# A planner that hands out PSUM banks by what open products can still finish, and a row factor applied in one instruction

## The chip, the cores and the metric

The kernel runs on one core of one Trainium2 chip. The metric is the device time of that core in microseconds. A core has a matmul engine (TensorE, PE), three engines for elementwise work (VectorE, DVE; ScalarE, ACT; GpSimd, POOL) and a queue from which transfers are issued (SyncE, SP). Each engine works through its own instructions in the order in which they were built, and waits at an instruction until the semaphores that it names are raised.

## The reference, cut to what matters

`x` has shape (128, 128, 256): 128 graphs of 128 nodes with 256 features each. `adj` holds one 128 x 128 matrix of 0 and 1 for each graph. Four layers follow each other, each with a residual and a layer norm:

```python
# layer 0: three steps of a gated graph network, the same GRU weights in all three
for i in range(3):
    m = einsum('bnd,de->bne', h, weight[i]);  aggr = einsum('bst,bsd->btd', A, m)
    h = gru_cell(aggr, h, w_ih, w_hh, b_ih, b_hh)
x = layernorm(x + h)
# layers 1 to 3: graph attention
Wh = x @ W.T;  e = leaky_relu(Wh @ a1 [:, None] + Wh @ a2 [None, :], 0.2)
alpha = softmax(where(adj == 0, very_negative, e));  x = layernorm(x + alpha @ Wh)
```

All of it is in fp32.

## The kernel before, in words

**Groups and steps.** Four graphs form a group (`G = 4`), 32 groups make the batch. `gru(g, stage)` emits the three GRU steps of a group, `gat(g, ...)` its three attention layers. In a GRU step the hidden state and the aggregate are held transposed, features in partitions. L630 makes the aggregate, and `strassen` forms the gate products at L572 with seven products of half blocks in place of eight. It is called twice in each step: `rz` has two gates and both sides (hidden and aggregate), so a product there is four matmuls; `nn` has two matmuls a product. The half blocks' sums come from `sums` (L542, on POOL or DVE).

**The banks of one form.** A call of `strassen` is called a form here. It opens three PSUM banks, `bx`, `by` and `bz`, of which there are five (tag `gate`). Products go on accumulating in a bank after what was in it has been copied out: `bx` takes A11, is copied by ScalarE (L638 for `rz`; L642 and L645, two instructions for two halves, for `nn`), takes S2, is copied again, and so on. VectorE adds two banks to a copied part (L577). A form that has begun thus needs all its three banks before it can give them back.

**Attention.** The score of a neighbour is a row that is spread over the partitions (L761 transposes it, L768 broadcasts it on POOL). L784 adds the mask and takes the maximum, L788 and L805 are the leaky ReLU and the exponential. The scores are then turned by a transpose over DMA: `turned` packs halves of the words (L466), issues the transpose from SP (L467) and unpacks (L470; the copies stand in the profile under L363, L365 and L461). L854 multiplies the scores with the features and L865 with the weights; L871 divides and adds the residual. Attention layers 1 to 3 do without a full layer norm between them: a factor for each row, `rstd`, is carried on, and in the last two of the three layers the turned scores are multiplied by it (`scaled`, L812 to L818). The last four groups (`LAST = 4`) transpose on TensorE instead of by DMA.

**The planner.** None of this is emitted directly. `plan.op(engines, fn, reads, writes, prio, ...)` records each operation with a price in ns for each engine that may do it. `order()` then plays the program through with those prices, picks for each operation an engine, a start and the slots of its buffers, and the instructions are emitted in the order of these starts. What matters here:

- On TensorE an operation counts as ready only when its inputs from other engines have been there for `MARGIN` ns by the plan.
- `own` holds, for a GRU part (first dictionary) and an attention part (second), how many slots of a tag are kept for the oldest part that still needs some; younger parts are given what is over. `spare` computes it.
- `PASSES` is the number of further rounds in which the due times found in the last round become priorities; the shortest plan of all rounds is kept.
- An operation with `port=BOTH` is not set on DVE while POOL holds the port by the plan, nor the other way.

A planned wait of TensorE is no instruction: on the chip each engine goes on as soon as the semaphores allow.

Of the kernel before, what the change touches and what calls it, by code (L numbers as in the profile page):

```python
# [13 lines left out]
ALU = mybir.AluOpType  # L14
AX = mybir.AxisListType

P = 128
D = 256
KC = D // P
G = 4  # L20
# [10 lines left out]
class Buf:  # L31


    def __init__(self, tag, *shape):
        self.tag, self.shape = tag, shape
        self.left = 0
        self.slot = None
        self.owner = None
        self.at = None


class Op:
# [7 lines left out]
class Plan:  # L50
# [10 lines left out]

    RUSH = 1.5
    RATHER = 600
    MARGIN = 50

    def __init__(self, slots, own):
        self.free = {t: list(range(n)) for t, n in slots.items()}
# [28 lines left out]
        self.ops.append(o)  # L96

    AHEAD = 1000000
    PASSES = 2

    def order(self):

# [41 lines left out]
    def once(self):  # L144
        import heapq
        for o in self.ops:
            o.missing, o.users = len(o.deps), []
            o.at, o.when = {}, {}
            for b in o.bufs:
                b.left, b.slot, b.owner = 0, None, None  # L150
        for o in self.ops:
            for b in o.bufs:
                b.left += 1
            for d in o.deps:
                d.users.append(o)
        idle = {"PE": 0, "ACT": 0, "DVE": 0, "POOL": 0, "SP": 0}
        ready = {e: [] for e in idle}
        done, seq, now = [], 0, 0
        arrived, started, running, leaving = [], set(), [], []
        held, coming, port = {}, {}, 0  # L160
        for o in self.ops:
            for b in o.bufs:
                if b.owner is None:
                    b.owner = o.group
                    coming[o.group, b.tag] = coming.get((o.group, b.tag), 0) + 1
        oldest = {t: min(g for g, t2 in coming if t2 == t) for t in self.free}

        def spare(g, t):

            while oldest[t] < g and not coming.get((oldest[t], t)):  # L170
                oldest[t] += 1
            first = oldest[t]
            if g <= first:
                return len(self.free[t])
            return len(self.free[t]) - max(0, min(self.own[first % 2].get(t, 1) - held.get((first, t), 0), coming[first, t]))

        def release(o):
            for e in o.engines:
                margin = self.MARGIN if e == "PE" else 0
                when = max([t + self.DELAY.get((e2, e), self.LATENCY[e2]) + (margin if e2 != e else 0) for e2, t in o.at.items()],  # L180
                           default=0)
                o.when[e] = max(when, o.earliest)
                heapq.heappush(arrived, (max(when, o.earliest), o.prio, e, o))

        for o in self.ops:
            if not o.missing:
                release(o)
        while len(done) < len(self.ops):
            while running and running[0][0] <= now:
                _, _, o, e = heapq.heappop(running)  # L190
                for b in o.bufs:
                    b.left -= 1
                    if not b.left:
                        heapq.heappush(leaving, (now + self.LATENCY[e] + o.lag, seq, b))
                        seq += 1
                for u in o.users:
                    u.missing -= 1
                    u.at[e] = max(u.at.get(e, 0), now + o.lag)
                    if not u.missing:
                        release(u)  # L200
            while leaving and leaving[0][0] <= now:
                b = heapq.heappop(leaving)[2]
                self.free[b.tag].append(b.slot)
                held[b.owner, b.tag] -= 1
            while arrived and arrived[0][0] <= now:
                _, prio, e, o = heapq.heappop(arrived)
                if o not in started:
                    heapq.heappush(ready[e], (prio, o))
            waited = {e: max(idle[e], min((i[1].when[e] for i in ready[e] if i[1] not in started), default=now)) for e in ("POOL", "DVE")}
            for e in ("PE", "ACT", "SP") + (("POOL", "DVE") if waited["POOL"] < waited["DVE"] else ("DVE", "POOL")):  # L210
                if idle[e] > now:
                    continue
                kept = []
                while ready[e]:
                    item = heapq.heappop(ready[e])
                    o = item[1]
                    if o in started:
                        continue
                    if e in o.port and port > now:
                        kept.append(item)  # L220
                        continue
                    if e == "POOL" and "DVE" in o.engines:
                        behind = max(idle["DVE"], now) + sum(
                            i[1].engines["DVE"] for i in ready["DVE"] if i[0] < item[0] and i[1] not in started)
                        if behind + self.RATHER + o.engines["DVE"] < max(now, port) + o.engines["POOL"]:
                            kept.append(item)
                            continue
                    need = [b for b in o.bufs if b.slot is None]
                    want = {}
                    for b in need:  # L230
                        want[b.tag] = want.get(b.tag, 0) + 1
                    if any(spare(o.group, t) < n for t, n in want.items()):
                        kept.append(item)
                        continue
                    for b in need:
                        b.slot = self.free[b.tag].pop(0)
                        held[b.owner, b.tag] = held.get((b.owner, b.tag), 0) + 1
                        coming[b.owner, b.tag] -= 1
                    started.add(o)
                    o.engine, o.start = e, now  # L240
                    idle[e] = now + o.engines[e]
                    if e in o.port and o.holds:
                        port = idle[e]
                    heapq.heappush(running, (idle[e], seq, o, e))
                    seq += 1
                    done.append(o)
                    break
                for item in kept:
                    heapq.heappush(ready[e], item)
            nxt = [t for t in idle.values() if t > now]  # L250
            if running:
                nxt.append(running[0][0])
            if arrived:
                nxt.append(arrived[0][0])
            if leaving:
                nxt.append(leaving[0][0])
            nxt = [t for t in nxt if t > now]
            if not nxt:
                if len(done) < len(self.ops):
                    raise RuntimeError("no operation can start")  # L260
                break
            now = min(nxt)
        self.span = max(idle.values())
        return done
# [3 lines left out]
def adj_resnorm_kernel(  # L268
# [14 lines left out]
    nc = tc.nc  # L283
# [9 lines left out]

    pools = {"gru": 4, "xs": 2, "am": 5, "k2": 28, "k4": 18, "f": 3, "mv": 4, "st": 6, "v": 36,
             "gate": 5, "bank": 3}
    own = ({"k2": 8, "k4": 8, "gate": 1, "bank": 0, "v": 5, "st": 0}, {"k2": 5, "k4": 2, "bank": 1, "v": 5, "st": 0})
    floats = {"gru": 0, "k4": 1024, "xs": 1024, "f": 128, "mv": 8, "st": 6, "v": 4}
    tags = {t: (n, floats.get(t, 512)) for t, n in pools.items()}
    U16 = mybir.dt.uint16
    BOTH = ("DVE", "POOL")  # L300
    LATER = (0.0, 1.5, -0.75, 0.25, 0, 0.0)
    plan = Plan({t: n for t, (n, _) in tags.items()}, own)
# [252 lines left out]
    def strassen(gates, kept, prio):  # L555

        bx, by, bz = Buf("gate", GN), Buf("gate", GN), Buf("gate", GN)
        o0, o1 = Buf("k4", 2, GN), Buf("k4", 2, GN)  # L560
        p1, u2, p5 = Buf("k2", GN), Buf("k2", GN), Buf("k2", GN)

# [174 lines left out]
    def gat(g, xc, no, stage):  # L737


        ve, rstd = None, None  # L740
        for l in range(3):
            prio = stage(g, STEPS + l)
# [4 lines left out]
            for h in (1, 0):  # L747
# [4 lines left out]
                if l:  # L752
                    plan.op({"DVE": 78}, lambda e, h=h, side=side, rstd=rstd: nc.vector.tensor_mul(
                        side(h), side(h), T(rstd)), reads=[((fi, f)[h], b) for b in range(G)] + [rstd],
                        writes=[((fi, f)[h], b) for b in range(G)], prio=prio, port=BOTH)
            e_, pT, y = Buf("k2", G, P), Buf("k2", G, P), Buf("k4", G, D)
# [52 lines left out]
            if by_xbar:  # L809
                turned(lambda e_=e_: T(e_), [(e_, b) for b in range(G)], pT, prio)  # L810
                if l:
                    def scaled(e, pT=pT, rstd=rstd):  # L812
                        for b in range(G):
                            if e == "DVE":
                                nc.vector.tensor_scalar(T(pT)[:, b, :], T(pT)[:, b, :], T(rstd)[:, b:b + 1], None, op0=ALU.mult)
                            else:
                                nc.scalar.mul(T(pT)[:, b, :], T(pT)[:, b, :], T(rstd)[:, b:b + 1])
                    plan.op({"DVE": 560, "ACT": 1010}, scaled, reads=[pT, rstd], writes=[pT], prio=prio, port=BOTH)  # L818
            else:
                b_ = bank()  # L820

# [118 lines left out]
```

## Time and profile before

| | us |
|---|---|
| median of 3 runs | 2532.05 (2530.18 to 2533.56) |
| the profiled execution, its own time | 2533.8 |
| its span, first to last instruction | 2532.0 |
| PE busy (matmul) / PEld busy (weight loads) | 2496.4 / 2209.9 |
| DVE / ACT / POOL busy | 2126.1 / 1957.9 / 958.4 |
| mean granted TensorE clock | 0.997 |

The busy time of an engine is the sum over its instructions, without overlaps. Matmuls are pipelined: one starts before the last has ended, and the ends are modelled, so that PE's busy time also hides short waits. An fp32 matmul shows in the profile as two passes with two weight loads, a transpose as one. A group's row gives the line, the engine, the operation, what it writes and reads, its shape, the count, the busy time and the mean of one, and then the idle time just ahead of it with what ended it. In the table of waits a row is: engine, tile, line, what it waited for, total us, number of times, longest. The profiled execution's own time is 1.8 us over its span and 1.75 us over the median of the runs.

### The profile page before, as it was taken

Reading aid. Unit: us, or ns where it says so; the run is one execution under the profiler, and the core shown is the slowest. Engines: PE = TensorE matmul, PEld = TensorE weight load, DVE = VectorE, ACT = ScalarE, POOL = GpSimd, SP = SyncE. Lnnn points to the kernel's source line nnn. Section 1 sums busy time; section 2 is a strip of 40 time slices with the busy share of each in tenths; the row PEclk is TensorE's granted clock in tenths of the full one; section 3 lists DMA queues with packets and bytes.
Section 4 is the critical chain, followed back from the end, with each engine's and each line's share of the span. In section 5 each row is a group of like instructions: output and inputs, shape, how many; then the busy total and the mean of one; then the engine's idle time right before and its main releaser. Section 6 shows DMA issues by size and latency. Waiting matters only on the chain.

```text
span 2532.0 us, 41142 instructions
## 1 busy us (share of the span) xinstructions
PE 2496.4 (99%) x13044; PEld 2209.9 (87%) x13044; DVE 2126.1 (84%) x6103; ACT 1957.9 (77%) x4799; POOL 958.4 (38%) x1204
## 2 busy tenths in 40 slices
PE   8999999999999999999999999999999999999988
PEld 6888888888888888888888888888888888888877
DVE  5688888988888988888888888988888888777887
ACT  5667877887788877878877887887887887666667
POOL 2333333443434434344444344534433433333211
PEclk9999999999999999999999999999999999999999
DMA  4222322322223322223232233323332232120101
GB/s 142 46 47 51 70 52 63 71 59 55 60 58 72 76 55 50 62 60 76 59 67 56 54 72 67 63 60 68 65 55 67 51 71 55 26 50 9 38 1 34
DMA packets 397466, 146.60 MB, mean 58 GB/s; under 512 B 330048, under 2 KB 395584, under 8 KB 397248
## 3 DMA queue, kind: packets, MB, share of 16 engines
q1 hardware_dynamic: 396816, 143.97, 26.0%
q8 instruction: 102, 1.67, 0.3%
q14 instruction: 116, 0.95, 0.1%
q10 hardware_dynamic: 432, 0.01, 0.0%
HBM read 45.89 MB, written 16.78 MB: 25 GB/s over the span
## 4 chain that ended last, share of the span: by engine, by line
PE 78%; DVE 9%; ACT 7%; DMA 3%; issue 2%; POOL 1%; POOLq 0%; ACTq 0%; SPq 0%; DVEq 0%
PE gate L572 56%; PE bank L865 10%; PE bank L854 6%; PE bank L630 5%; DMA k<-k 2%; DVE nobody L749 2%; DVE k L577 1%; ACT k L363 1%; ACT k L461 1%; DVE k L871 1%; DMA xs<-in_x_dram 1%; ACT k L656 1%; ACT k L805 1%; DVE k L365 1%; DVE k L784 1%
## 5 line engine op out<-in xcount | busy, mean ns | idle before, releaser
L572 PE MATMUL gate<-k,whs 128*128 128x256 f32 x4032 | 1206.3, 381 | 10.7 <-ACT k L638 5.7
L572 PE MATMUL gate<-k,wcs 128*128 128x256 f32 x4032 | 1200.2, 379 | 0.0
L572 PEld LDWEIGHTS gate<-k,wcs 128*128 128x128 f32 x4032 | 766.6, 190 | 104.4
L572 PEld LDWEIGHTS gate<-k,whs 128*128 128x128 f32 x4032 | 740.0, 190 | 120.3 <-ACT k L638 11.4
L542 POOL TENSOR_TENSOR k<-k,k 128x256 f32<-128x256 f32 x491 | 410.6, 853 | 322.1 <-DVE k L695 102.3
L577 DVE TENSOR_TENSOR k<-gate,k 128x512 f32<-128x512 f32 x576 | 391.0, 684 | 148.0 <-PE gate L572 89.3
L489 POOL TENSOR_TENSOR v<-v,neghalf 128x4 f32<-128x4 f32 x128 | 154.3, 1206 | 554.9 <-DVE v L527 300.9
L865 PE MATMUL bank<-gwT,k 128*128 128x256 f32 x1536 | 349.4, 380 | 1.7 <-DVE k L365 1.2
L865 PEld LDWEIGHTS bank<-gwT,k 128*128 128x128 f32 x1536 | 290.0, 190 | 43.8 <-DVE k L365 3.1
L749 DVE SCALAR_TENSOR_TENSOR nobody<-k,wa 128x256 f32<-128x256 f32 x768 | 315.3, 448 | 4.5 <-ACT k L508 3.9
L461 ACT COPY k<-k 128x1024 uint16<-128x1024 uint16 x217 | 251.8, 1163 | 59.0 <-DMA k<-k 56.5
L656 ACT ACTIVATE k<-k,brz 128x256 f32<-128x256 f32 (+1 forms) x384 | 226.6, 623 | 40.5 <-DVE k L577 40.1
L363 ACT COPY k<-bank 128x512 f32<-128x512 f32 (+1 forms) x280 | 145.3, 523 | 126.1 <-PE bank L761 57.0
L542 POOL TENSOR_TENSOR k<-k 128x256 f32<-128x256 f32 x158 | 136.3, 863 | 238.6 <-DVE k L695 68.8
L690 POOL TENSOR_TENSOR k<-k,k 128x512 f32<-128x512 f32 x85 | 113.1, 1332 | 295.4 <-ACT k L685 221.2
L516 ACT ACTIVATE nobody<-k 128x256 f32<-128x256 f32 x384 | 156.8, 411 | 75.9 <-DVE k L871 74.9
L638 ACT COPY k<-gate 128x512 f32<-128x512 f32 x288 | 166.3, 581 | 59.3 <-PE gate L572 58.4
L768 POOL PARTITION_BROADCAST k<-k x336 | 150.5, 546 | 156.2 <-ACT k L363 102.5
L871 DVE SCALAR_TENSOR_TENSOR k<-bank,v,k 128x256 f32<-128x256 f32 x384 | 167.2, 476 | 44.3 <-PE bank L865 42.6
L363 ACT COPY k<-k 128x1024 uint16<-128x1024 uint16 x161 | 168.1, 1046 | 45.3 <-DVE k L695 43.7
L854 PEld LDWEIGHTS bank<-k,k 128*128 128x128 f32 x1536 | 187.9, 193 | 11.0 <-ACT k L363 1.9
L854 PE MATMUL bank<-k,k 128*128 128x128 f32 x1536 | 190.9, 277 | 3.9 <-ACT k L363 1.4
(100 smaller groups left out, 3274.6 us busy)
## 6 DMA issues: line engine op xcount, KB each, us to landing
xs<-in_x_dram SPq DMA_DIRECT2D x32, 512.0 KB, 4.1
k<-in_x_dram SPq DMA_DIRECT2D x32, 512.0 KB, 4.1
out_dram<-k SPq DMA_DIRECT2D x32, 512.0 KB, 3.0
am<-in_adj_dram SPq DMA_DIRECT2D x32, 256.0 KB, 3.0
k<-k SPq DMA_TRANSPOSE x310, 3.1
k<-in_gnn_wT_dram SPq DMA_DIRECT2D x3, 256.0 KB, 4.9
k<-in_w_ihT_dram SPq DMA_DIRECT2D x2, 384.0 KB, 5.6
k<-in_w_hhT_dram SPq DMA_DIRECT2D x2, 384.0 KB, 6.4
```

The costliest lines, as they stand in the source:

```text
L363: nc.scalar.copy(dst, src)
L461: nc.scalar.copy(flat().bitcast(U16).rearrange("p (q h) -> p q h", h=2), T(rows).bitcast(U16).rearrange("p (h q) -> p q h", h=2))
L516: plan.op({"ACT": 400}, lambda e, b=b: nc.scalar.activation(next(nobody[0]), T(y)[:, b, :], AF.Square, accum_out=T(ss)[:, b:b + 1]), reads ...
L542: nc.vector if e == "DVE" else nc.gpsimd).tensor_tensor(T(t)[:, j, :], a(), b(), ALU.subtract),
L572: nc.tensor.matmul(T(dst)[:, j * H:(j + 1) * H], T(w)[:, m, gt, :], moving(m, ms)[1](), start=first and n == 0, stop=n == len(todo) - 1, s ...
L577: plan.op({"DVE": 602}, lambda e: nc.vector.tensor_add(T(o)[:, :, j * H:(j + 1) * H], T(b_).rearrange("p (g n) -> p g n", g=2), T(part).re ...
L638: plan.op({"ACT": 475}, lambda e: nc.scalar.copy(T(dst), T(src)), reads=[src], writes=[(dst, 0), (dst, 1)], prio=prio)
L656: nc.scalar.activation(T(o)[:, gt, n0:n1], src(), AF.Tanh, bias=brz[:, gt * KC + c:gt * KC + c + 1], scale=0.5)
L749: plan.op({"DVE": 345}, lambda e, b=b, h=h, l=l, side=side, xc=xc: nc.vector.scalar_tensor_tensor(next(nobody[1]), T(xc)[:, b, :], 1.0, T( ...
L854: nc.tensor.matmul(T(b_)[:, b * P:(b + 1) * P], T(xc)[:, b, c * P:(c + 1) * P], T(pT)[:, b, :], start=True, stop=True)
L865: nc.tensor.matmul(T(b_)[:, (b - b0) * D:(b - b0 + 1) * D], T(aT[k])[:, b * P:(b + 1) * P], T(gwT)[:, l, k, :], start=(k == 0), stop=(k == ...
L871: nc.vector.scalar_tensor_tensor(T(y)[:, b, :], T(b_)[:, (b - b0) * D:(b - b0 + 1) * D], T(rden)[:, b:b + 1], T(xc)[:, b, :], op0=ALU.mult ...
```

## The change

Three things are edited.

The planner gets a test for deadlock. The three banks of one form are marked as a unit. Before a bank is handed out, `safe` asks whether, afterwards, the open forms could still all be finished one after the other with the banks that are free or come free; if not, the operation is kept back. If nothing else can go on, one operation may take slots although they were set aside for an older part (`forced`).

The numbers of the planner change: `MARGIN` from 50 to 250, `PASSES` from 2 to 1, and in `own` for a GRU part `k4` from 8 to 6 and `gate` from 1 to 2, for an attention part `k2` from 5 to 3.

The row factor of the turned scores, four instructions for four graphs before, is one `tensor_tensor` with the factor spread along the rows when it falls to DVE or POOL. POOL is new among its engines. On ACT it stays four instructions. The prices are written anew.

```diff
-    MARGIN = 50
+    MARGIN = 250
-    PASSES = 2
+    PASSES = 1
...
+        units = {}
+
+        def safe(bufs):
+
+            claim = {u: list(v) for u, v in units.items()}
+            free = {}
+            for b in bufs:
+                if b.unit is None:
+                    continue
+                free.setdefault(b.tag, len(self.free[b.tag]))
+                c = claim.setdefault(b.unit, [b.tag, 0, len(b.unit)])
+                free[b.tag] -= 1
+                c[1] += 1
+                c[2] -= 1
+            for t in free:
+                left = [c for c in claim.values() if c[0] == t]
+                while left:
+                    c = next((c for c in left if c[2] <= free[t]), None)
+                    if c is None:
+                        return False
+                    free[t] += c[1]
+                    left.remove(c)
+            return True
...
-                    if any(spare(o.group, t) < n for t, n in want.items()):
+                    if any((len(self.free[t]) if forced else spare(o.group, t)) < n for t, n in want.items()):
                         kept.append(item)
                         continue
+                    if not safe(need):
+                        kept.append(item)
+                        continue
+                    forced = False
...
             if not nxt:
-                if len(done) < len(self.ops):
+                if len(done) == len(self.ops):
+                    break
+                if forced:
                     raise RuntimeError("no operation can start")
-                break
+                forced = True
+                continue
...
-    own = ({"k2": 8, "k4": 8, "gate": 1, "bank": 0, "v": 5, "st": 0}, {"k2": 5, "k4": 2, "bank": 1, "v": 5, "st": 0})
+    own = ({"k2": 8, "k4": 6, "gate": 2, "bank": 0, "v": 5, "st": 0}, {"k2": 3, "k4": 2, "bank": 1, "v": 5, "st": 0})
...
         bx, by, bz = Buf("gate", GN), Buf("gate", GN), Buf("gate", GN)
+        bx.unit = by.unit = bz.unit = (bx, by, bz)
...
                     def scaled(e, pT=pT, rstd=rstd):
-                        for b in range(G):
-                            if e == "DVE":
-                                nc.vector.tensor_scalar(T(pT)[:, b, :], T(pT)[:, b, :], T(rstd)[:, b:b + 1], None, op0=ALU.mult)
-                            else:
+                        if e == "ACT":
+                            for b in range(G):
                                 nc.scalar.mul(T(pT)[:, b, :], T(pT)[:, b, :], T(rstd)[:, b:b + 1])
-                    plan.op({"DVE": 560, "ACT": 1010}, scaled, reads=[pT, rstd], writes=[pT], prio=prio, port=BOTH)
+                        else:
+                            (nc.vector if e == "DVE" else nc.gpsimd).tensor_tensor(
+                                T(pT), T(pT), T(rstd).unsqueeze(2).to_broadcast([P, G, P]), ALU.mult)
+                    plan.op({"DVE": 602, "POOL": 1235, "ACT": 1168}, scaled, reads=[pT, rstd], writes=[pT], prio=prio, port=BOTH)
```

The lines of the changed kernel stand 41 lower than before from `exitstack` on, 42 from the mark of the unit on, and 43 after the row factor.

More of the change, by code (lines that the diff above doesn't have):

```diff
@@ L39, in __init__ @@
         self.at = None
+        self.unit = None
 class Op:
@@ L159, in once @@
         arrived, started, running, leaving = [], set(), [], []
-        held, coming, port = {}, {}, 0
+        held, coming, port, forced = {}, {}, 0, False
         for o in self.ops:
@@ L204, in once @@
                 held[b.owner, b.tag] -= 1
+                if b.unit is not None:
+                    c = units[b.unit]
+                    c[1] -= 1
+                    if not c[1] and not c[2]:
+                        del units[b.unit]
             while arrived and arrived[0][0] <= now:
@@ L231, in once @@
                         want[b.tag] = want.get(b.tag, 0) + 1
-                    if any(spare(o.group, t) < n for t, n in want.items()):
+                    if any((len(self.free[t]) if forced else spare(o.group, t)) < n for t, n in want.items()):
                         kept.append(item)
                         continue
+                    if not safe(need):
+                        kept.append(item)
+                        continue
+                    forced = False
                     for b in need:
                         b.slot = self.free[b.tag].pop(0)
+                        if b.unit is not None:
+                            c = units.setdefault(b.unit, [b.tag, 0, len(b.unit)])
+                            c[1] += 1
+                            c[2] -= 1
                         held[b.owner, b.tag] = held.get((b.owner, b.tag), 0) + 1
```

## The prediction

> **What bounds the kernel now.** First the page: busy time of each engine, then the chain that ended last.
>
> ```profile
> PE 2496.4 (99%) x13044; PEld 2209.9 (87%) x13044; DVE 2126.1 (84%) x6103; ACT 1957.9 (77%) x4799; POOL 958.4 (38%) x1204
> ...
> PE 78%; DVE 9%; ACT 7%; DMA 3%; issue 2%; POOL 1%; POOLq 0%; ACTq 0%; SPq 0%; DVEq 0%
> ```
>
> TensorE is the bound, but 99% is a modelled figure, so I take its floor from start times. In the timeline, successive passes of 256 columns start 0.2157 us apart where nothing is waited for, passes of 128 columns 0.111, single-pass transposes 0.109. Counts from the groups: (8064 gate + 1536 L865) x 0.2157 = 2070.7; (1536 L854 + 1536 L630) x 0.111 = 341.0; 300 transposes x 0.109 = 32.7; weights at the start 20.7. Floor **2465 us** of a span of 2532.0. The other 67 us is all that an order of work can touch. Second, where it lies, by stretches of 80 us:
>
> ```profile
> core 0: us, PE busy (x) PEld busy (x) DVE busy (x) ACT busy (x) POOL busy (x), PEclk, DMA share, GB/s
> 0.00:80.00 80.00, 72.20 (x330) 59.35 (x330) 44.27 (x92) 43.44 (x78) 21.13 (x30) 0.98 0.39 112
> ...
> 1200.00:1280.00 80.00, 77.74 (x403) 68.03 (x402) 67.54 (x221) 63.20 (x157) 36.89 (x47) 1.00 0.29 67
> ...
> 2400.00:2480.00 80.00, 73.34 (x389) 62.67 (x388) 71.75 (x308) 54.48 (x177) 10.03 (x9) 0.96 0.00 1
> 2480.00:2560.00 80.00, 42.71 (x261) 37.20 (x260) 39.37 (x196) 38.40 (x154) 8.65 (x8) 0.95 0.08 27
> ```
>
> I added up, from the start times, every distance beyond the pace: **head** (to 80 us) 5.1 before the first matmul and 7.9 after; **middle** (80 to 2400) 26.1, of which 46 waits over 0.06 us hold 18.4, plus about 0.1 each lost inside the next pass (4.6), the rest being small ones; **tail** 15.6, and 8.9 after the last matmul; with 3 us of rounding that is the 67. The window at 1200 is the worst of the middle; the tail's first window has DVE busy 71.75 of 80, so VectorE bounds it for some 40 us. Third, who ends TensorE's waits:
>
> ```profile
> PE gate L572 <- ACT k L638: 5.7, 8, 2.0
> PE bank L480 <- DMA xs<-in_x_dram: 5.1, 1, 5.1
> PE gate L572 <- ACT k L645: 4.2, 7, 1.8
> ```
>
> L480 is the first load. The two others are a gate bank whose partial product ScalarE has not copied out yet. The longest, in the timeline:
>
> ```profile
> 1245.21 0.45 ACT L642 ACTIVATE k<-gate,bhn 128x256 f32<-128x256 f32 x1
> 1245.57 1.03 ACT L363 COPY k<-k 128x1024 uint16<-128x1024 uint16 x1
> ...
> 1246.50 0.37 ACT L645 COPY k<-gate 128x256 f32<-128x256 f32 x1
> ...
> 1246.92 0.70 PE L572 MATMUL gate<-k,whs 128*128 128x256 f32 x2 [1.80 <-ACT k L645]
> ```
>
> An unrelated copy of 1.03 us stands in ScalarE's queue between the two halves of one bank's eviction; the matmul behind them starts 1.8 us late.
>
> **What the skill says.** The Trainium skill, Perfetto Trace Analysis, "Identifying the Most-Contended Engine", calls matmul busy time a bad measure of distance to the roofline; agreed: the busy 2496.4 hides 31 us over the floor of 2465. The same page, "Matmuls": independent matmul groups should rotate through different PSUM banks so that an eviction overlaps the next group; the waits above are the cases where too little stood between. "Optimizing Scalar/DVE Operations": each DVE instruction carries a data-access overhead, so grouping helps a saturated engine; agreed, four of 128 columns took 1.05 us (17.9 us for 17 pieces), one of 512 columns 0.69 to 0.73. GPSIMD Engine Reference, "4.1 Engine selection": two-input elementwise about 2x slower than VectorE; agreed, 1332 ns against 734 for L690 below.
>
> **The change part by part.** TensorE's 6674 instructions are the same in both built orders; only their order and what stands between them differ.
>
> (1) Unit test and forced grants. With the test left out of the changed kernel the built order is the same, and so it is with PASSES at 2: in this case the test refuses nothing. Worth 0, both ends 0.
>
> (2) The scaling in one instruction. Before, 56 pieces (28 groups, 2 layers): 17 on DVE, 39 on ACT.
>
> ```profile
> L690 POOL TENSOR_TENSOR k<-k,k 128x512 f32<-128x512 f32 x85 | 113.1, 1332 | 295.4 <-ACT k L685 221.2 <-issue 57.8 <-DVE k L577 7.9
> L690 DVE TENSOR_TENSOR k<-k,k 128x512 f32<-128x512 f32 x107 | 78.3, 734 | 27.5 <-ACT k L685 26.8
> L817 ACT ACTIVATE k<-k,v 128x128 f32<-128x128 f32 x156 | 49.9, 395 | 2.2 <-DVE k L365 1.0
> L815 DVE TENSOR_SCALAR k<-k,v 128x128 f32<-128x128 f32 x68 | 17.9, 328 | 3.8 <-ACT k L461 3.8
> ```
>
> After, 4 on DVE, 24 on POOL, 28 on ACT. DVE 17.9 -> 2.9; ACT 39 x 1.28 = 49.9 -> 35.8; POOL 0 -> 24 x 1.33 = 32. No row shows POOL with a factor spread along rows: I bound it by 1.28 (L690's median) and 1.8 (its longest), and take 1.33. Its reader is L854 on TensorE. By data alone there are 5.1 us to spare, but in the built order, the same way in 24 turns, the piece is taken up only 0.86 to 2.59 us before L854, after a transpose by DMA and its unpacking (L470); 1.33 and 0.12 for the signal leave -0.6 to 1.1. For it speaks that the planner counts 3.49 us for such a DMA, which lands in 3.1, and reserves 0.25: together 0.6 against the 0.1 that POOL takes over its price. I take 0; bounds 0 and 24 x 0.6 = +14. Behind the piece in POOL's queue stand a power (L489), a subtraction (L690) and the next broadcasts (L768), whose readers are VectorE's, off the path. The old prices were wrong (planned 0.56 on DVE against 1.05, 1.01 on ACT against 1.28), the new ones are near (0.60, 1.17, 1.24).
>
> (3) What else moves: 42 L690 from POOL to DVE, 24 L542 sums from DVE to POOL, 42 16-bit copies from DVE to ACT, 22 row copies from ACT to DVE. DVE: -15.0 + 42 x 0.73 - 24 x 0.59 - 42 x 0.75 + 22 x 0.28 = -24 us; ACT: -14 + 35 x 1.04 + 7 x 1.16 - 6 = +24; POOL: -56 + 32 + 20 = -4. DVE stays at 83% and ACT at 78%, so none becomes the bound; SP's 453 DMAs are unchanged in number.
>
> (4) The order, set by MARGIN, the own counts and the new prices together (with any one of the three taken back it is another order). After group 4 each group follows the last in the same way: the last matmuls of successive groups lie 75.6 us of TensorE work apart, with a standard deviation of 0.2; before, of 7.7. For every product I counted the matmul work that stands between it and the TensorE work its data or bank come from, less what lies between at the planner's prices: its **spare**. A bank's ACT copy costs 0.220 + 0.475 + 0.190 = 0.885; one product of four matmuls, 1.727, gives 0.842 of spare. In the middle (1906 operations) those with under 1 us fall from **419 to 293**, under 0.5 from **17 to 3**; those whose last input is the pair L642/L645, at 0.96, from 70 to 3. With a copy set between that pair, the least spare is 0.96 before (the case of 1246) and 1.82 after.
>
> Middle: 25 of the 46 waits (9.2 us) stand at products with under 1 us. Without the L645 kind and with a third fewer: 4.0. The other 21 (9.2 us) come from late queues; a reserve of 0.25 us in place of 0.05 takes 0.2 from each, which leaves some 5, and prices nearer the truth a little more: 4.0. Loss inside the next pass: 46 -> 22 waits, 4.6 -> 2.2. Together 23.0 -> 10.2: **-12.8**. These are the unsure terms; bounds -20 (nearly no waits left) and +15 (below).
>
> Head: equal to 47 us. Then two products of group 1 waited 2.13 + 0.69 and 0.21 + 0.88 us, each with 0.84 spare; in the new order they have 5.5 and 2.6. **-3.5** (bounds -3.9, 0).
>
> Tail: VectorE bounds it, with 84 us of work at the planner's prices left when TensorE has 76 left, against 83 in the new order. But the negative spares in the last 108 us sum to 11.1 against 9.4: **+1.7** (bounds -3, +6).
>
> Sum: -12.8 - 3.5 + 1.7 = -14.6, from the profiled execution's 2533.8 to 2519.2; the median of the runs lies 1.75 below that execution, so 2517.5, **2518**.
>
> **Rivals.** A, slower: a wait that recurs. In a periodic order any wait that the planner misjudges returns in all 25 turns. Candidates are POOL's piece ahead of L854 (up to 0.6) and the eight products a turn with under 1 us spare, behind L577, L638, L857 and L632. At 1.5 us a turn: +37.5 - 23.0 - 3.5 + 1.7 = +12.7, 2545; it decides from (23.0 + 3.5 - 1.7)/25 = 1.0 us a turn, and exceeds 0.2% from 1.2. For it: POOL's pieces run 8 to 22% over their prices (1332 against 1235, 0.84 against 0.69). Against: of 307 products with 0.75 to 1 us spare only 18 waited, 7.6 us in all.
>
> B, no change: late queues, not the order, make the waits; they move elsewhere and the middle keeps 23. Then -3.5 + 1.7: 2530. For it: half the waits stand where the data had over 1 us to spare.
>
> C: the middle gains as forecast, the tail, bound by VectorE, loses 6: 2522.
>
> D: the edits reach no instruction; the built orders exclude it, except for (1).
>
> **How the numbers follow.** A measurement of this kernel can tell about 0.2%, 5 us. Forecast 0.55, A 0.17, B 0.18, C 0.10. Faster by over 0.2% (below 2527.0): forecast, C and a little of B, 0.70; within: most of B, 0.14; slower (over 2537.1): A, 0.16. The range takes the lower bounds of middle and head on one side (2509) and reaches into A on the other (2540).
>
> **What would show it.** Right: TensorE's waits on L645 nearly gone and those on L638 below 3 us; no window between 80 and 2400 with TensorE under 78.5; windows 75.6 us apart alike; the start past 50 us without the 2 us wait. Wrong: one pair of lines in the table of waits with 20 or more entries (A); the sum of TensorE's waits still near 20 (B); the tail's loss over 20 us up to the last matmul (C).

## The result and the profile after

The changed kernel takes **2515.05 us** (median of 4 runs, 2514.19 to 2516.06) against 2531.76 for the kernel before beside it (4 runs, 2530.18 to 2533.56). The ratio is 0.9934, with a 95% interval from 0.9917 to 0.9951. The forecast was 2518. The span of the profiled execution fell from 2532.0 to 2513.4 us.

First the page after: busy time of each engine, and the chain that ended last. TensorE's share of the chain has risen from 78% to 86%, so fewer of its waits belong to other engines. ScalarE took on 24 us of work and VectorE lost 45; neither is the bound, before or after.

```profile
PE 2485.2 (99%) x13044; PEld 2210.3 (88%) x13044; DVE 2081.4 (83%) x6033; ACT 1982.0 (79%) x4782; POOL 932.4 (37%) x1210
...
PE 86%; DVE 7%; ACT 3%; DMA 2%; issue 2%; POOL 0%; POOLq 0%; ACTq 0%; DVEq 0%
```

Then the busy times by stretches of 80 us (columns as before). At 1200, where the worst window of the middle stood (77.74), TensorE now has 79.56, and the lowest value anywhere between 80 and 2400 is 79.25. The first window gained 1 us, the last but one lost 1 (73.34 before), and the last is shorter because the work ends sooner.

```profile
0.00:80.00 80.00, 73.15 (x350) 60.62 (x351) 49.34 (x97) 46.74 (x84) 22.42 (x30) 1.00 0.44 121
...
640.00:720.00 80.00, 79.25 (x418) 70.33 (x418) 67.37 (x197) 66.27 (x157) 30.90 (x41) 1.00 0.28 62
...
1200.00:1280.00 80.00, 79.56 (x417) 70.94 (x416) 67.51 (x192) 63.92 (x151) 30.26 (x40) 1.00 0.29 60
...
2400.00:2480.00 80.00, 72.28 (x420) 62.42 (x419) 75.12 (x381) 61.01 (x228) 12.05 (x11) 0.98 0.00 1
2480.00:2560.00 80.00, 23.67 (x140) 20.10 (x139) 17.93 (x78) 22.57 (x85) 5.15 (x5) 0.95 0.08 27
```

Third, TensorE's waits. L680 is the old L638, L687 the old L645. The two kinds that carried 5.7 and 4.2 us are at 1.0 and 1.8. What is left is the first load, waits of the tail (L763, L897, L908, L867), and short ones behind L687 and L619, none longer than 0.7 us.

```profile
PE bank L521 <- DMA xs<-in_x_dram: 5.9, 2, 5.1
PE bank L763 <- DVE k L737: 2.8, 1, 2.8
PE bank L897 <- DVE k L872: 2.1, 2, 1.1
PE gate L614 <- DVE k L619: 1.8, 6, 0.6
PE gate L614 <- ACT k L687: 1.8, 3, 0.7
...
PE gate L614 <- ACT k L680: 1.0, 2, 0.7
```

The start times of the passes, with every distance beyond the pace added up as in the prediction, say where the 18.6 us of span came from: head 13.1 -> 9.6, middle 26.2 -> 9.8, tail up to the last matmul 15.6 -> 16.8, behind it 8.8 in both. (Here and below the tail is the last 121 us up to the last matmul's start, and the middle reaches from 80 us to there, so that kernels of different lengths can be compared.) **The gain lies in the middle.**

### The profile page after: what moved, and what is told of

It is laid out like the page before. It is cut to its first block, busy times and chain, and to the rows that moved or that the text cites. A ratio compares the mean times of both kernels' runs of the same rounds, so it can differ in the third digit from the quotient of the medians.

```text
span 2513.4 us, 41086 instructions
## 1 busy us (share of the span) xinstructions
PE 2485.2 (99%) x13044; PEld 2210.3 (88%) x13044; DVE 2081.4 (83%) x6033; ACT 1982.0 (79%) x4782; POOL 932.4 (37%) x1210
## 3 DMA queue, kind: packets, MB, share of 16 engines
q1 hardware_dynamic: 396816, 143.97, 25.9%
## 4 chain that ended last, share of the span: by engine, by line
PE 86%; DVE 7%; ACT 3%; DMA 2%; issue 2%; POOL 0%; POOLq 0%; ACTq 0%; DVEq 0%
PE gate L614 61%; PE bank L908 11%; PE bank L672 6%; PE bank L897 6%; DMA k<-k 2%; DVE nobody L791 1%; DVE k L619 1%; DVE k L914 1%; DMA xs<-in_x_dram 1%; DVE k L714 0%; ACT k L698 0%; ACT k L502 0%; ACT k L404 0%; PE bank L458 0%; ACT k L847 0%
## 5 line engine op out<-in xcount | busy, mean ns | idle before, releaser
L619 DVE TENSOR_TENSOR k<-gate,k 128x512 f32<-128x512 f32 x576 | 388.0, 684 | 155.0 <-PE gate L614 100.8
L530 POOL TENSOR_TENSOR v<-v,neghalf 128x4 f32<-128x4 f32 x128 | 138.9, 1086 | 658.1 <-DVE v L568 367.1
L908 PE MATMUL bank<-gwT,k 128*128 128x256 f32 x1536 | 349.0, 380 | 1.1 <-ACT k L404 0.9
L908 PEld LDWEIGHTS bank<-gwT,k 128*128 128x128 f32 x1536 | 290.3, 190 | 42.6 <-ACT k L404 2.6
L502 ACT COPY k<-k 128x1024 uint16<-128x1024 uint16 x224 | 259.6, 1160 | 32.9 <-DMA k<-k 32.7
L698 ACT ACTIVATE k<-k,brz 128x256 f32<-128x256 f32 (+1 forms) x384 | 233.2, 627 | 38.6 <-DVE k L619 38.6
L583 POOL TENSOR_TENSOR k<-k 128x256 f32<-128x256 f32 x181 | 142.2, 786 | 230.5 <-DVE k L737 173.9
L406 DVE COPY k<-bank 128x512 f32<-128x512 f32 (+1 forms) x244 | 145.4, 597 | 84.8 <-PE bank L897 73.5
L680 ACT COPY k<-gate 128x512 f32<-128x512 f32 x288 | 167.0, 581 | 61.5 <-PE gate L614 59.4
L727 ACT ACTIVATE k<-k,bi 128x512 f32<-128x512 f32 x192 | 138.5, 722 | 97.7 <-DVE k L718 77.6
L404 ACT COPY k<-k 128x1024 uint16<-128x1024 uint16 x189 | 198.4, 1050 | 16.9 <-DVE k L737 15.7
L810 POOL PARTITION_BROADCAST k<-k x336 | 170.1, 606 | 67.1 <-ACT k L404 64.2
L897 PEld LDWEIGHTS bank<-k,k 128*128 128x128 f32 x1536 | 185.6, 193 | 9.4 <-DVE k L872 2.6
```

Source lines behind the costliest of these rows:

```text
L404: nc.scalar.copy(dst, src)
L502: nc.scalar.copy(flat().bitcast(U16).rearrange("p (q h) -> p q h", h=2), T(rows).bitcast(U16).rearrange("p (h q) -> p q h", h=2))
L583: nc.vector if e == "DVE" else nc.gpsimd).tensor_tensor(T(t)[:, j, :], a(), b(), ALU.subtract),
L619: plan.op({"DVE": 602}, lambda e: nc.vector.tensor_add(T(o)[:, :, j * H:(j + 1) * H], T(b_).rearrange("p (g n) -> p g n", g=2), T(part).re ...
L680: plan.op({"ACT": 475}, lambda e: nc.scalar.copy(T(dst), T(src)), reads=[src], writes=[(dst, 0), (dst, 1)], prio=prio)
L698: nc.scalar.activation(T(o)[:, gt, n0:n1], src(), AF.Tanh, bias=brz[:, gt * KC + c:gt * KC + c + 1], scale=0.5)
```

## The experiments

Theory 1: MARGIN, the own counts and the new form of the factor matter only together, because only together do they make the planner's order repeat from group to group. Theory 2: the larger MARGIN carries the gain. Theory 3: the single instruction and its prices do. Each was run beside the kernel before on one chip, but not all on the same one: there were three, and on them the kernel before took 2531.6, 2532.5 and 2532.1 us. So the ratios can be compared from row to row; a difference of about 1 us between two times cannot.

| kernel | us | ratio to before, 95% | head | middle | tail | distances of groups, standard deviation | products under 1 us spare |
|---|---|---|---|---|---|---|---|
| before | 2531.76 | | 13.1 | 26.2 | 15.6 | 7.7 | 419 |
| MARGIN alone | 2544.25 | 1.0047 [1.0035, 1.0060] | 9.5 | 37.8 | 17.1 | 8.7 | 384 |
| own counts alone | 2552.84 | 1.0078 [1.0065, 1.0090] | 10.5 | 37.5 | 25.1 | 7.1 | 440 |
| factor alone | 2540.67 | 1.0032 [1.0023, 1.0042] | 11.9 | 37.7 | 11.9 | 5.7 | 432 |
| all but MARGIN | 2541.99 | 1.0038 [1.0024, 1.0052] | 10.3 | 35.9 | 17.4 | 6.3 | 443 |
| all but own counts | 2546.22 | 1.0053 [1.0041, 1.0066] | 9.4 | 39.8 | 19.4 | 7.0 | 393 |
| all but the factor | 2534.14 | 1.0009 [1.0000, 1.0017] | 9.9 | 25.6 | 18.8 | 4.9 | 387 |
| **changed** | 2515.05 | 0.9934 [0.9917, 0.9951] | 9.6 | 9.8 | 16.8 | 0.2 | 293 |
| changed, factor in four instructions, same order | 2514.52 | 0.9929 [0.9917, 0.9942] | 9.3 | 10.1 | 16.3 | 0.2 | 293 |
| changed, MARGIN 600 | 2529.53 | 0.9990 [0.9983, 0.9996] | 8.8 | 26.1 | 16.7 | 3.5 | 256 |
| changed, gate count 1 | 2521.47 | 0.9959 [0.9947, 0.9972] | 11.4 | 11.1 | 19.2 | 0.4 | 405 |
| changed, 600 from group 26 | 2516.51 | 0.9937 [0.9925, 0.9950] | 9.4 | 11.3 | 16.6 | 0.9 | 280 |
| changed, 600 from group 27 | 2518.60 | 0.9946 [0.9934, 0.9958] | 9.5 | 11.8 | 18.3 | 0.4 | 273 |
| changed, POOL's pieces three times | 2541.70 | 1.0040 [1.0027, 1.0052] | 9.1 | 35.9 | 17.7 | 0.2 | 293 |

Head, middle and tail are us lost on TensorE in one profiled execution each, from start times, with the 3 us of rounding that the prediction names taken out of the middle. The last two columns are read from the built orders: how far the last matmuls of successive groups lie apart, and the spare as the prediction defines it. The kernel with POOL's pieces three times multiplies 24 pieces by the cube of the factor, so it computes something else; it is there for its time.

### One edit alone

```diff
-    MARGIN = 50
+    MARGIN = 250
```

> The kernel before with MARGIN 250 in place of 50, nothing else. Theory 1 (the three edits together make the order, no single one does): the built order stays irregular and 384 products of the middle have under 1 us spare (419 before, 293 after), so part of the waits go: 2519 to 2530. Theory 2 (the reserve of 0.25 us alone carries it): 2513 to 2518. Theory 3 (the factor's instruction and its prices carry it): 2529 to 2534.

Measured 2544.25: slower than before, and outside what any of the theories gave, theory 1 too. The middle lost 37.8 us instead of 26.2, though fewer products have under 1 us spare. Two of its windows of 80 us (columns as above) hold TensorE at 77.57 and 76.62, and the waits, in the second fence, are spread over many pairs of lines:

```profile
1360.00:1440.00 80.00, 77.57 (x400) 68.22 (x400) 66.28 (x199) 56.75 (x140) 26.41 (x35) 1.00 0.31 60
1760.00:1840.00 80.00, 76.62 (x404) 67.97 (x403) 70.32 (x207) 63.67 (x154) 33.00 (x42) 1.00 0.28 63
```

```profile
PE gate L572 <- DVE k L577: 5.5, 9, 1.2
PE bank L854 <- ACT k L461: 4.1, 4, 2.0
PE gate L572 <- ACT k L638: 4.1, 7, 0.8
```

ScalarE is busy 56.75 of the 80 us in the first and VectorE 66.28: neither is short of time over the whole window. Theory 2 falls.

```diff
-    own = ({"k2": 8, "k4": 8, "gate": 1, "bank": 0, "v": 5, "st": 0}, {"k2": 5, "k4": 2, "bank": 1, "v": 5, "st": 0})
+    own = ({"k2": 8, "k4": 6, "gate": 2, "bank": 0, "v": 5, "st": 0}, {"k2": 3, "k4": 2, "bank": 1, "v": 5, "st": 0})
```

> The kernel before with the own counts of after (k4 6, gate 2; k2 3), nothing else. Theory 1: 440 products under 1 us spare and a worse tail (negative spares sum to 14.9 us against 9.4): 2530 to 2540. Theory 2 and theory 3: no gain, 2529 to 2536.

Measured 2552.84, the slowest of all and above every range. The tail is much of it, as the sum of negative spares had said (25.1 us lost against 15.6), but the middle lost 11 us more as well.

```diff
-                            if e == "DVE":
-                                nc.vector.tensor_scalar(T(pT)[:, b, :], T(pT)[:, b, :], T(rstd)[:, b:b + 1], None, op0=ALU.mult)
...
+                            (nc.vector if e == "DVE" else nc.gpsimd).tensor_tensor(
+                                T(pT), T(pT), T(rstd).unsqueeze(2).to_broadcast([P, G, P]), ALU.mult)
...
-                    plan.op({"DVE": 560, "ACT": 1010}, scaled, reads=[pT, rstd], writes=[pT], prio=prio, port=BOTH)
+                    plan.op({"DVE": 602, "POOL": 1235, "ACT": 1168}, scaled, reads=[pT, rstd], writes=[pT], prio=prio, port=BOTH)
```

> The kernel before with the row factor in one instruction, POOL allowed, new prices, nothing else (8 pieces on POOL, 19 on DVE, 29 on ACT). Theory 1: 432 products under 1 us spare, order irregular: 2526 to 2534. Theory 2: 2529 to 2534. Theory 3: 2513 to 2520.

Measured 2540.67, again slower and above every range. Theory 3 in its simple form falls: prices nearer the truth did not by themselves give a better order. Theory 1 was right that no single edit gives the gain but missed all three times, by 7 to 14 us: it did not foresee how much a single edit costs. Its ranges in the next section were set with these results known.

### One edit taken back

Here the changed kernel has MARGIN, the own counts, or the factor with its prices as before; the diffs are those above, reversed.

> The changed kernel with MARGIN back at 50 (own counts and factor as changed). Order irregular (6.3 us), 443 products under 1 us spare. Theory 1 (all three together make the repeating order, and that is the gain): 2530 to 2550. Theory that own counts and factor carry part of the gain: 2518 to 2526.

> The changed kernel with the own counts back (MARGIN and factor as changed). Order irregular (standard deviation of the groups' distances 7.0 us), 393 products under 1 us spare. If the repeating order is the gain: 2530 to 2550, as with the other irregular orders (2541 to 2553 with one edit, 2542 with MARGIN back). If MARGIN and factor carry it between them: 2515 to 2522.

> The changed kernel with the row factor as before, four instructions on DVE or ACT at the old prices (MARGIN and own counts as changed). Order irregular (4.9 us), 387 products under 1 us spare. If the repeating order is the gain: 2528 to 2548. If MARGIN and own counts carry it between them: 2515 to 2522.

Measured 2541.99, 2546.22 and 2534.14: all within what the repeating order as the cause had given, none near 2515 to 2526. With the three of the last section, the six kernels between before and changed are all slower than before, or equal to it (the last, 1.0009 with an interval that begins at 1.0000). No sum of single effects gives the changed kernel. The first half of theory 1 is shown: only together do the three gain. That the repeating order is why is its second half, and these runs do not test it apart.

### The instruction by itself

```diff
-                            (nc.vector if e == "DVE" else nc.gpsimd).tensor_tensor(
-                                T(pT), T(pT), T(rstd).unsqueeze(2).to_broadcast([P, G, P]), ALU.mult)
+                        elif e == "DVE":
+                            for b in range(G):
+                                nc.vector.tensor_scalar(T(pT)[:, b, :], T(pT)[:, b, :], T(rstd)[:, b:b + 1], None, op0=ALU.mult)
+                        else:
+                            for b in range(G):
+                                nc.gpsimd.tensor_tensor(T(pT)[:, b, :], T(pT)[:, b, :],
+                                                        T(rstd)[:, b:b + 1].to_broadcast([P, P]), ALU.mult)
```

> The changed kernel with the same plan and order, but each piece on DVE or POOL issued as four instructions of 128 columns instead of one of 512. In the trace of the changed kernel a POOL piece ends 1.45 us before its reader in 22 of 24 turns, so theories 1 and 2 (order alone): four on POOL take 1.2 to 2.0 us in place of 1.04, still inside: 2514 to 2517. Theory 3 (the single instruction is what helps): over 2520.

Measured 2514.52, the same as the changed kernel. The order is the same instruction for instruction, apart from these pieces. A piece on POOL now takes 1.47 us in place of 1.04 and ends 1.03 us before its reader in place of 1.45; no engine shows a wait for it. That the factor is applied in one instruction is worth nothing in time here; its prices, and POOL among its engines, are what the planner sees.

### Is it that the order repeats, or that products have more to spare?

Two kernels part these. MARGIN 600 gives more products enough spare, in an order that is not the same from group to group; a gate count of 1 gives an order that repeats in each group, with about as many tight products (under 1 us spare) as before.

```diff
-    MARGIN = 250
+    MARGIN = 600
```

> The changed kernel with MARGIN 600 in place of 250. Its order is not the same from group to group (the distances of successive groups have a standard deviation of 3.5 us against 0.2), but only 256 products of the middle have under 1 us spare (293 in the changed kernel). If the repeating order is what helps: 2525 to 2545, like the three edits made alone (2541 to 2553). If the spare of single products is what helps: 2510 to 2517.

```diff
-    own = ({"k2": 8, "k4": 6, "gate": 2, "bank": 0, "v": 5, "st": 0}, {"k2": 3, "k4": 2, "bank": 1, "v": 5, "st": 0})
+    own = ({"k2": 8, "k4": 6, "gate": 1, "bank": 0, "v": 5, "st": 0}, {"k2": 3, "k4": 2, "bank": 1, "v": 5, "st": 0})
```

> The changed kernel with the own count of gate banks back at 1. Its order repeats from group to group (standard deviation 0.4), with 405 products under 1 us spare, nearly as many as before (419), and 51 of 56 factor pieces on POOL. If the repeating order is what helps: 2512 to 2521. If the spare of single products is what helps: 2526 to 2540.

Measured 2529.53 and 2521.47. The middle decides against the spare: 26.1 us lost with 256 tight products, 11.1 with 405.

It does not decide for repetition as such. The order of MARGIN 600 repeats too, but only every seven groups: in the built order every TensorE operation of groups 11 to 17 stands at the same distance, 534.5 us, from its like seven groups later. The trace shows it. These are all the waits of a gate product on L687 in that kernel, seven groups apart:

```profile
785.52 0.70 PE L614 MATMUL gate<-k,whs 128*128 128x256 f32 x2 [1.57 <-ACT k L687]
...
1325.36 0.70 PE L614 MATMUL gate<-k,whs 128*128 128x256 f32 x2 [1.57 <-ACT k L687]
...
1862.45 0.70 PE L614 MATMUL gate<-k,whs 128*128 128x256 f32 x2 [1.56 <-ACT k L687]
```

So an order can repeat, some of its waits with it, and lose as much as the kernel before. What the quick orders have is narrower: each group like the last. The same two windows of the second kernel, to be set beside those of MARGIN alone:

```profile
1360.00:1440.00 80.00, 80.00 (x420) 71.61 (x419) 65.56 (x202) 69.57 (x165) 33.21 (x44) 1.00 0.30 60
1760.00:1840.00 80.00, 80.00 (x428) 71.82 (x427) 66.00 (x190) 69.94 (x164) 33.58 (x45) 1.00 0.27 60
```

ScalarE is busier there than in any window shown of the kernels that lose much, and TensorE shows no idle time; elsewhere in the middle its lowest window has 78.59. So a busy ScalarE alone does not make the waits. Whether the share of work does is a rival that no run tests: the planner also gives VectorE less to do in the orders that repeat in each group. Over the whole span it is busy 2031 to 2093 us in these and 2110 to 2150 in the eight others, ScalarE 1972 to 2059 and 1920 to 1961. Against this rival speaks that among the eight the order is not that of the load: the one with the least VectorE time (2110, all but own counts) lost the most in the middle, 39.8 us, and two of those with much (2141 and 2144, all but the factor and MARGIN 600) the least, 25.6 and 26.1.

The time came out half a microsecond above the range; its span, 5.6 us longer than the changed kernel's, has 1.8 of that in the head, 2.4 in the tail and 1.3 in the middle.

### What a wait that recurs costs

```diff
+                            for _ in range(3 if e == "POOL" else 1):
```

> The changed kernel, same plan and order, with every piece of the row factor that falls to POOL issued three times (so 24 pieces carry the cube of the factor). In the trace of the changed kernel a piece takes 1.04 us and ends 1.45 us before its reader L897 in 22 turns. If that is the true cover, 2.08 us more overrun it by 0.63 and by the crossing between the engines, some 0.7 to 0.9 in 24 turns: 15 to 22 us longer, 2530 to 2537. If the path has slack elsewhere, that is if L897 can be late without harm: 2515 to 2520.

This is rival A made on purpose, at the place that the prediction named. First, from the timeline of the changed kernel, one turn as it is (start, us, engine, line): the unpacking on VectorE, the piece on POOL, and its reader, which starts 1.47 us after the piece has ended.

```profile
1271.12 0.75 DVE L406 COPY k<-k 128x1024 uint16<-128x1024 uint16 x1
1272.01 1.04 POOL L859 TENSOR_TENSOR k<-k,v 128x512 f32<-128x512 f32 x1 [5.60 <-DVE k L406]
...
1274.52 0.72 PE L897 MATMUL bank<-k,k 128*128 128x128 f32 x5
```

With three pieces in a row, the timeline of the same turn and the row in the table of TensorE's waits (total, times, longest):

```profile
1283.06 3.28 POOL L860 TENSOR_TENSOR k<-k,v 128x512 f32<-128x512 f32 x3 [5.63 <-DVE k L406]
...
1286.39 2.05 PE L898 MATMUL bank<-k,k 128*128 128x128 f32 x16 [0.69 <-POOL k L860]
```

```profile
PE bank L898 <- POOL k L860: 18.7, 24, 1.8
```

Measured 2541.70, 26.7 us over the changed kernel where 15 to 22 were expected. By start times the matmul comes about 0.84 us late in 21 of the 24 turns and 1.3 to 2.0 us in the other three, and loses 0.1 more in its next pass: 25.1 us of the 26.1 that the middle lost. What the piece has to spare is real: it ends 2.24 us later (3.28 against 1.04) and its reader is 0.84 late, so 1.40 us was the cover, the 1.45 less the 0.05 that pass between its end and the reader's start. That a wait in every turn costs its full length, as rival A assumed, holds. Where A put the break-even does not: 1.0 us a turn there, because it counted on all 23.0 us of the other waits to go. Measured, the gain of 16.7 us is used up by 0.7 us in each of 24 turns, and 1.1 us a turn (26.7 over 24) left the kernel 0.4% slower than before.

### A better version?

The tail was left. From group 26, or 27, on the reserve was set to 600 ns, which leaves the repeating order up to about there and takes the sum of the tail's negative spares from 11.1 to 6.4 and 7.3 us.

```diff
-                margin = self.MARGIN if e == "PE" else 0
+                margin = (self.MARGIN if o.group < 52 else 600) if e == "PE" else 0
```

> The changed kernel, but from group 26 on TensorE's inputs have to be there 600 ns by the plan, in place of 250. The order repeats up to there (standard deviation 0.9 over groups 4 to 25); 280 products under 1 us spare (293); the negative spares of the last 108 us sum to 6.4 us (11.1). If the repeating order and the sum of negative spares in the tail are what counts: middle as in the changed kernel, tail 3 to 5 us shorter, 2509 to 2514. If a larger reserve costs by itself, as 600 throughout seemed to: 2516 to 2524.

> The same from group 27 on: standard deviation 0.4, 273 products under 1 us spare, negative spares of the tail 7.3 us. If the repeating order and the tail's negative spares are what counts: 2510 to 2515. If a larger reserve costs by itself: 2516 to 2524.

Measured 2516.51 and 2518.60 (the second with 54 for 52). Neither beats the changed kernel: the tail loses 16.6 and 18.3 us against 16.8, and the middle 1.5 to 2.0 more. The sum of negative spares does not foretell the tail to a few us. Both times lie in the range given for a reserve that costs by itself, but by their intervals neither kernel differs from the changed one. No kernel tried is faster than it; 2514.52 is the same by its interval.

## Why the prediction was right, and where its reasons were not

The forecast was 2518 and the time 2515.05, with all of the gain in head and middle, as foretold. That the sum came so near is in part luck: the largest term rests on a step that the experiments contradict (under **Middle**).

**What bounds the kernel.** The split into head, middle and tail says where the gain lies: -3.5 - 16.4 + 1.2 = -18.7 against -18.6 of span. That the three add up is only arithmetic, since the passes are the same in both kernels; it does not test the floor of 2465 us. The smallest span of any run here, 2512.4, is 47 us above it.

**Unit test, forced grants, PASSES.** Taken at 0 because the built order is the same without them. The programs are then the same too, so there was nothing to measure. The part of the change that the title names first has no share in the gain.

**The factor.** Taken at 0, measured at 0 (2514.52 with four instructions in the same order). Its size was off: POOL took 1.04 us a piece, below the lower bound of 1.28, and the time to spare was 1.45 us where I had -0.6 to 1.1.

```profile
L859 POOL TENSOR_TENSOR k<-k,v 128x512 f32<-128x512 f32 x24 | 25.0, 1040 | 138.1 <-DVE k L406 123.9 <-ACT k L502 8.5 <-ACT k L687 5.7
L732 POOL TENSOR_TENSOR k<-k,k 128x512 f32<-128x512 f32 x43 | 55.6, 1293 | 69.3 <-ACT k L727 68.1 <-DVE k L859 1.2
```

**What else moves.** ScalarE +24 forecast, +24.1 measured. VectorE -24 forecast, -44.7 measured: beyond the moved pieces, its instructions are shorter on average (L734, the old L692, at 696 ns in place of 736, with medians of 680 and 684). GpSimd -4 forecast, -26 measured: 7 from the cheaper pieces, 15 from shorter powers (138.9 in place of 154.3 us). Neither engine became the bound; whether the lighter VectorE helped the waits, no run tells.

**Head.** -3.5 forecast, -3.5 measured. **Tail.** +1.7 forecast, +1.2 measured, though the runs with a reserve of 600 in the tail show that the sum it was read from is no sure guide.

**Middle.** -12.8 forecast, -16.4 measured. L638's waits went as foretold (from 5.7 to 1.0); L645's fell from 4.2 to 1.8, which is not yet the "nearly gone" of the prediction. The sum of all TensorE's waits in the table is 19.1 us, from 25.9, so by the letter the sign of B ("still near 20") is met; but most of what is left lies in the head and the tail, and in the middle, by start times, waits over 0.06 us fell from 18.4 to 5.9. So the middle's gain is real. But **the step from spare to waits failed**. I had reasoned that fewer tight products, and a reserve larger by 0.2 us, each take their part off the waits. MARGIN alone lowers the tight products from 419 to 384 and loses 11.6 us more in the middle; MARGIN 600 has the fewest tight products, 256, and loses as much as the kernel before; a gate count of 1 has 405 and loses 11.1. By the prediction's reasoning MARGIN alone should have gained. What goes with a small loss is that each group's order is like the last's: the four orders with a standard deviation under 1 us lose 9.8 to 11.8 us in the middle (POOL's pieces three times apart, which have the changed kernel's order and a wait put into it), the eight with 3.5 us or more lose 25.6 to 39.8. The four are not four independent cases: the two with a reserve of 600 at the end have, in the middle of the batch, the plan of the changed kernel (in group 15 every operation stands where it stands there), so there are two such orders against eight. The prediction saw the repeating order, but entered it as a danger (rival A).

Which property of these orders makes the waits short is **not settled**; that it is the repetition is argued from which kernels are quick, and the order of MARGIN 600, which repeats every seven groups and loses 26.1, speaks against it in its general form. Another reading is that an order is the same in each group just when the planner finds hardly any gap on TensorE, and that the missing gaps are what counts: by the plan's own starts TensorE has 2 gaps over 0.06 us in the changed kernel's middle, 0.9 us in all, and 3.2 to 5.0 us in the three other repeating orders, against 26 gaps and 11.4 us before, 27 and 19.2 with MARGIN 600, and 15 to 29 us in the others. This parts the orders that lose little from those that lose much as well as repetition does, MARGIN 600 included. But among the eight that lose much the planned gaps do not rank the loss (11.4 us of gaps go with 26.2 lost, 19.6 with 25.6, 14.9 with 35.9), and of the 46 waits measured before only 5 stand where the plan had a gap (10 of 28 with MARGIN 600), so a wait on the chip is mostly not the plan's gap come true; that TensorE, which on the chip does not pause where the plan does, then runs ahead of the other engines would fit, and was not tried.

**Rivals.** A did not occur by itself; that a wait in each turn costs its full length was right, its break-even of 1.0 us a turn was too high (0.7 by the measured gain). B (late queues make the waits, and they only move) is nearest to what the irregular orders did, though most of them lost time by it. C did not occur. The runs with one edit taken back show how near the sign was: had any one of the three been missing, the time would have been the same or up to 0.5% longer.

## What to carry to other kernels

Where a planner writes the order, the effects of its knobs need not add up: three edits that each cost 0.3 to 0.8% alone gained 0.66% together, so test them as a set and look at the order that comes out before arguing from a knob's meaning. In this loop over equal groups, orders that are the same in each group and have hardly any planned gap on TensorE lost less than half of what the others lost; both can be told from the built order without a run, though which of them matters is open. In such an order a wait of 0.7 us in each turn costs as much as the whole gain, so measure what the last piece ahead of the bounding engine has to spare (here 1.45 us) and keep it.

## What the runs showed of the hardware that I had not expected

On GpSimd a product of 128 x 512 with a factor for each row of 128, spread by the access pattern, takes 1.04 us (median of 24, L859), against 1.27 us for a subtraction of two operands of full size (median of 43, L732). The operation differs as well as the operand, and no run parts the two. In four instructions of 128 columns the product takes 1.47 us, start to end. On VectorE the two cost about the same, 692 and 687 ns (medians of L859 and L732). A matmul that started late behind GpSimd's three pieces lost another 0.10 us in its next pass, in all 24 turns.
